# Two layers of masked graph attention: both layers' scores as neighbours, and two vector steps in other places

## The chip, the cores and the metric

The kernel runs on one core of a Trainium2 chip. The metric is the device time of one execution in microseconds (us). A core has five engines that run side by side, each through its own list of instructions in order, and wait for each other by semaphores: TensorE (PE in the profile; its weight loads are PEld), VectorE (DVE), ScalarE (ACT), GpSimd (POOL) and SyncE (SP), which issues the transfers.

## The reference

There are 64 graphs of 256 nodes with 512 features. Layer 0 normalizes the rows, applies a ReLU, maps the rows (`m`), and makes two things from `m` for each of 8 heads of width 64: a softmax over scaled scores of `q` and `k`, and a 0/1 adjacency from cosines of the unit vectors of `m`. Their product weighs the messages. Layer 1 is masked attention with 4 heads. Both layers add to the input. Cut to what matters here:

```python
h = relu(layernorm(x))
m = h @ map_w.T + map_b                        # split into 8 heads of 64
n = m / max(norm(m), 1e-8)
cos_adj = (n @ n.T) * ~mask > 0.1              # "cosines", "unit vectors"
q, k = m @ q_w.T + q_b, m @ k_w.T + k_b
p = softmax(where(mask, -1e10, q @ k.T / 8)) * keep
adj = cos_adj * p
x = x + relu((adj @ (h @ gcn_map_w.T + gcn_map_b)) @ gcn_W.T / (adj.sum(-1) + 1))
h = relu(layernorm(x))                         # layer 1: 4 heads of 64
x = x + softmax(where(mask, q1 @ k1.T / 8, -big)) @ v1 @ Wo + bo
```

Here `mask` is true where a pair is left out in layer 0, and layer 1 takes the pairs the other way round.

## The kernel before

Everything is in 32-bit floats. The kernel is one long list written out by hand: `manual_schedule` keeps each engine's instructions in the order of the Python calls. The function `period(i)` is called for i = 0 to 64. In one period four graphs are at work at different stages: `b` (graph i-1) does its layer 1 attention, `g` (graph i) its layer 0 attention and the projections of its layer 1, `nx` (graph i+1) its layer 0 map, messages, queries and keys, and `n2` (graph i+2) is normalized and turned. In periods 1 to 62 `b`, `g` and `nx` all exist; period 0 has no `b`, period 63 no `nx`, and period 64 only `b`.

Some parts that the change and the profile's rows touch:

- **Products with seven instead of eight blocks.** `seven_products` (L260 to L327) multiplies 2 x 2 blocks with seven products, and is a generator: each `next` issues one step. Three of the products go one after the other into the same PSUM bank, called `z`. Each of the later two may start only when VectorE has read what the bank held: after the first, `out(0, 0, ...)` (L301, shown as mT<-p_m_z,u2p_m for the map), after the second, the sum u4 (L321, uup_m for the map, uup_q for the queries). The map, the messages, the queries and the keys are such products (p_m, p_s, p_q, p_k).
- **Scores.** `products` (L401) makes scores (tile sc) for two heads at a time from 64 rows each, into two PSUM banks; `exps` (L408, ScalarE) empties them into e. All PSUM tiles come from one ring of eight banks in the order of allocation.
- **Masks and half sums.** `masked` (VectorE) multiplies the exponentials by the mask: L415 in layer 1, L417 in layer 0, four calls of 128 x 1024 each period. `halves` (GpSimd, L421) adds the two halves of each, for the sums of the softmax. `off_edges` does both for the listed pairs of heads of layer 0.
- **Cosines.** `spread` sends the inverse norms over DRAM to all partitions of nT, `units` (VectorE, L384) multiplies them with mT in place, and `cosines` (L438) multiplies nT with itself. Only the upper blocks are computed; `far_off` (L448, L451) applies them, sends the block off the diagonal through a transposing transfer, and `far_back` (L463, "turned pass") applies the turned block later, followed by an add on GpSimd (L465).

In `period` before, the order around the change was: scores of layer 1, their masks and half sums; first step of the map (`next(m)`, p_m into bank p_m_24); scores of layer 0; first step of the messages (p_s); masks of the first two pairs of heads; second step of the map, which holds the first z product; third mask; the further steps; cosines. The unit vectors of `nx` were made at the very end of the period before, and the turned passes stood each ahead of a step of the queries or messages.

Of the kernel before, what the change touches and what calls it, by code (L numbers as in the profile page):

```python
# [147 lines left out]
def fast_path(ctx, tc, a, w, chk, out):  # L148
# [8 lines left out]
    H0, NKC = D // DH, D // P  # L157
# [16 lines left out]
    def bank(name, shape=(P, 2, S), dtype=F32):  # L174
        return ring.tile(list(shape), dtype, tag="bank", name=name)
# [175 lines left out]
    def halved(g):  # L351
        g.left_m = left_factors(g.mT, "sm", g.i)
# [29 lines left out]
    def units(g):  # L382

        nc.vector.tensor_mul(g.nT, g.nT, g.mT)  # L384
# [10 lines left out]
    def products(rows, cols, c, name):  # L395

        ps = [bank(f"{name}_{s}", [P, NT, S]) for s in range(2)]
        for j in range(NT):
            for s in range(2):
                h = slice(s * DH, (s + 1) * DH)  # L400
                nc.tensor.matmul(ps[s][:, j, :], rows[h, c, j * P:(j + 1) * P], cols[h, c, :], start=True, stop=True)  # L401
        return ps

    def exps(ps, name):

        e = sb2.tile([P, 2, NT * S], F32, tag="e", name=f"e{name}", bufs=6)
        for s, p in enumerate(ps):
            nc.scalar.activation(e[:, s, :], p.rearrange("p j q -> p (j q)"), AF.Exp, scale=SCALE)  # L408
        return e

    def masked(e, mask, edges):

        m = mask.rearrange("p j q -> p (j q)")[:, None, :].to_broadcast([P, 2, NT * S])
        if edges:
            nc.vector.scalar_tensor_tensor(e, m, 0.5, e, op0=ALU.is_lt, op1=ALU.mult)  # L415
        else:
            nc.vector.tensor_mul(e, e, m)  # L417

    def halves(e, name):
        d = sb2.tile([P, 2, S], F32, tag="d", name=f"d{name}", bufs=6)  # L420
        nc.gpsimd.tensor_add(d, e[:, :, :S], e[:, :, S:])  # L421
        return d
# [133 lines left out]
    def period(i):  # L556
        g = graphs.get(i) if i < B else None
        b, nx, n2 = graphs.get(i - 1), graphs.get(i + 1), graphs.get(i + 2)
        def off_edges(cs):
            for c in cs if g else ():  # L560
                masked(g.e[c], g.mask, edges=False)
                g.d[c] = halves(g.e[c], f"0_{i}_{c}")


        if b:
            b.e1 = [exps(products(b.k1T, b.q1T, c, f"sc1_{b.i}_{c}"), f"1_{b.i}_{c}") for c in range(NIC)]
            for c in range(NIC):
                masked(b.e1[c], b.mask, edges=True)
            if b.last:
                for t in range(NT):  # L570
                    values_in(b, t)
            else:
                b.d1 = [halves(b.e1[c], f"1_{b.i}_{c}") for c in range(NIC)]
        if nx:
            m, s = mapped(nx), messages(nx)
            next(m)
        if g:
            for c in range(NKC):
                g.e[c] = exps(products(g.kT, g.qT, c, f"sc0_{i}_{c}"), f"0_{i}_{c}")
        if nx:  # L580
            next(s)
        off_edges((0, 1))
        if nx:
            next(m)
        off_edges((2,))
        if nx:
            next(m)
            next(s)
            next(m)
            halved(nx)  # L590

        if g:
            for c in range(NKC):
                far_off(g, c, cosines(g, c))
                if c == 0:
                    off_edges((3,))
            for c in range(NKC):
                far_added(g, c)
        if n2:
            shifts(n2, f"0_{n2.i}")  # L600
        if nx:
            q = queries(nx)
            next(q)
            next(s)
        if n2:
            sent(n2, f"0_{n2.i}", 0)
        if nx:
            next(q)
            squares(nx)
            next(s)  # L610
        if n2:
            sent(n2, f"0_{n2.i}", 1)
        for c in range(NKC):
            if g:
                far_back(g, c)
            if nx and c < 3:
                next((q, s, q)[c])
        if nx:
            lengths(nx, norms(nx))

        if i == 0:
            w.finish_seven(w.wqk1)
        if b:
            sums1(b)
            values1(b)
        if g:
            g.avs = sb1.tile([P, NKC, S], F32, tag="wide", name=f"avs{i}")
            g.sms = sb1.tile([P, S], F32, tag="sms", name=f"sms{i}")
            values(g, 0)
            values(g, 1)  # L630
            sums(g)
        if n2:
            joined(n2, f"0_{n2.i}")
            join(n2, 0)
        if nx:
            k = keys(nx)
            next(k)
        if b:
            nc.scalar.activation(b.rz, b.rz, AF.Copy, accum_out=chk[:, b.i, 3:4])
        if g:  # L640
            sums_back(g)
            heads_back(g)
        if n2:
            join(n2, 1)
        if nx:
            next(k)
        if n2:
            edges(n2)
        if b:
            divided(b)  # L650
        if g:
            moments(g, f"1_{i}")
        if nx:
            next(k)
        if g:
            deviations(g)
        if g:
            normalized(g, f"1_{i}")
        if nx:
            nc.scalar.activation(nx.rn, nx.rn, AF.Sqrt)  # L660

        nc.scalar.activation(spare[:, 1:], spare[:, :1], AF.Exp)
        if b:
            for t in range(NT):
                result(b, t)
                if b.last:
                    nc.sync.dma_start(out=out_t[b.i][:, t], in_=b.xs[:, t])
            if not b.last:
                nc.sync.dma_start(out=out_t[b.i], in_=b.xs)
        if i + 3 < B:  # L670
            graphs[i + 3] = load(i + 3)
        if g:
            g.h1T = turned(g, f"1_{i}", "wide")
            j = queries_keys1(g)
            for t in range(NT):
                nc.gpsimd.tensor_add(g.xs[:, t, :], g.xs[:, t, :], w.bo_b)
        if nx:
            next(k)
        if g:
            next(j)  # L680
        if nx:
            nc.vector.reciprocal(nx.rn, nx.rn)
            spread(nx)
        if g:
            next(j)
        if g:
            next(j)
            if not g.last:
                values_in(g, 0)
            next(j)  # L690
        if n2:
            n2.left_h = left_factors(n2.hT, "sh", n2.i)
        if i + 3 < B:
            moments(graphs[i + 3], f"0_{i + 3}")
        if g and not g.last:
            values_in(g, 1)
        if nx:
            units(nx)

    def normal_input(g):  # L700
        g.hT = turned(g, f"0_{g.i}", "hT")
# [2 lines left out]
    with tc.manual_schedule():  # L704
        spare = small.tile([P, 2], F32, tag="spare", name="spare", bufs=1)
        nc.vector.memset(spare, 0.0)
        graphs = {0: load(0)}
        w.load_map()
        gws = [sb2.tile([P, 2, D], F32, tag="e", name=f"gw{k}", bufs=6) for k in range(2)]
        w.load_folded(gws)  # L710
        w.load_scores()
        graphs.update({n: load(n) for n in range(1, min(3, B))})
        w.load_rest()

        def normal(n):
            moments(graphs[n], f"0_{n}")
            deviations(graphs[n])
            normalized(graphs[n], f"0_{n}")

        g = graphs[0]  # L720
        normal(0)
        normal_input(g)
        edges(g)
        w.finish_seven(w.wm)
        m = mapped(g)
        next(m)
        next(m)
        w.fold(gws, bank, w.put_seven)
        next(m)
        w.finish_seven(w.wq)  # L730
        next(m)
        halved(g)
        squares(g)
        w.finish_seven(w.wk)
        q, k, s = queries(g), keys(g), messages(g)
        next(q)
        lengths(g, norms(g))
        w.fold_bias(sb2.tile([P, NKC, P], F32, tag="xn", name="gbb"), bank)
        w.finish_seven(w.wc)
        for step in (k, q, k, q, k, q, k):  # L740
            next(step)
        nc.scalar.activation(g.rn, g.rn, AF.Sqrt)
        nc.vector.reciprocal(g.rn, g.rn)
        spread(g)
        if B > 1:
            edges(graphs[1])
            normal(1)
        nc.scalar.activation(spare[:, 1:], spare[:, :1], AF.Exp)
        for _ in range(5):
            next(s)  # L750
        units(g)
        if B > 1:
            normal_input(graphs[1])
        if B > 2:
            moments(graphs[2], "0_2")
        for i in range(B + 1):
            period(i)
# [298 lines left out]
```

## Time and profile before

| what | value |
|---|---|
| time, median of 3 runs (lowest, highest) | 3695.86 us (3694.76, 3696.32) |
| span of the profiled execution | 3695.8 us |
| one period in the middle, from score product to score product | 56.58 us |
| TensorE busy | 3651.0 us (99%) |
| VectorE, GpSimd, ScalarE busy | 75%, 64%, 52% |
| mean granted TensorE clock | 0.996 |

A row of the timeline gives the start, the length, the engine, the line of the kernel, the operation, what it writes and reads, the shapes, and how many instructions in a row are merged; in brackets stands how long the engine was idle before, and whom it waited for. Matmuls overlap, so a group's cost is the distance from its start to the start of the next group. A 32-bit matmul is recorded as two passes.

### The profile page before, as it was taken

How to read it: one execution, taken by the hardware profiler on the slowest of the kernel's cores; microseconds unless marked ns; L12 is line 12 of the kernel's file. 1: busy time of each engine (PE TensorE's matmuls, PEld its weight loads, DVE VectorE, ACT ScalarE, POOL GpSimd, SP SyncE). 2: the span in 40 equal slices, each digit the busy share in tenths (PEclk: the TensorE clock that was granted, in tenths of full speed). 3: DMA queues.
4: the chain of work that ended last, by engine and by line, in shares of the span. 5: the costliest groups of instructions: out<-in, count | busy, mean ns of one | idle time of the engine just before them, and what ended most of it. 6: DMA issues, size and time to landing. Idle time of an engine off the chain costs nothing.

```text
span 3695.8 us, 76415 instructions
## 1 busy us (share of the span) xinstructions
PE 3651.0 (99%) x29153; PEld 3091.7 (84%) x29153; DVE 2774.1 (75%) x5288; ACT 1904.1 (52%) x4480; POOL 2348.0 (64%) x2044
## 2 busy tenths in 40 slices
PE   7999999999999999999999999999999999999997
PEld 7888888888888888888888888888888888888885
DVE  6777777777777777777877777777777777777775
ACT  3555555555555555555555555555555555555543
POOL 3667566666665665666766666666666667566663
PEclk9999999999999999999999999999999999999998
DMA  3111211211211112112112121121121112211211
GB/s 109 46 50 50 57 44 54 60 42 53 56 47 54 45 53 59 43 53 59 43 54 51 50 57 44 53 60 43 52 56 46 54 47 52 58 43 53 60 29 35
DMA packets 361008, 191.71 MB, mean 52 GB/s; under 512 B 272449, under 2 KB 326977, under 8 KB 360641
## 3 DMA queue, kind: packets, MB, share of 16 engines
q1 hardware_dynamic: 358368, 186.76, 19.0%
q8 instruction: 232, 3.80, 0.4%
q14 instruction: 136, 1.11, 0.1%
q10 hardware_dynamic: 2272, 0.04, 0.0%
HBM read 94.67 MB, written 34.34 MB: 35 GB/s over the span
## 4 chain that ended last, share of the span: by engine, by line
PE 96%; DVE 1%; DMA 1%; POOL 0%; issue 0%; ACT 0%; SPq 0%; DVEq 0%; ACTq 0%; POOLq 0%
PE sc L401 9%; PE av L428 9%; PE p_k L276 6%; PE p_q L276 6%; PE p_m L276 6%; PE p_qk L276 6%; PE p_s L271 6%; PE p_o L553 6%; PE p_v L520 6%; PE p_q_z L276 5%; PE co L438 5%; PE p_qk_z L276 5%; PE p_k_z L276 5%; PE p_m_z L276 5%; PE p_s_z L271 4%; PE sm L481 2%
## 5 line engine op out<-in xcount | busy, mean ns | idle before, releaser
L421 POOL TENSOR_TENSOR d<-e 128x512 f32<-128x512 f32 x382 | 716.2, 1900 | 199.5 <-DVE e L415 191.6
L408 ACT ACTIVATE e<-sc 128x512 f32<-128x512 f32 x768 | 389.9, 620 | 382.1 <-PE sc L401 375.6
L417 DVE TENSOR_TENSOR e<-e,mask 128x1024 f32<-128x1024 f32 x256 | 465.0, 1836 | 55.0 <-ACT e L408 55.0
L506 POOL TENSOR_TENSOR xs<-xs,o 128x512 f32<-128x512 f32 x128 | 188.5, 1494 | 385.5 <-DVE o L504 385.5
L465 POOL TENSOR_TENSOR d<-d,e 128x512 f32<-128x512 f32 x252 | 321.3, 1275 | 170.9 <-DVE e L463 169.2
L254 POOL TENSOR_TENSOR sh<-hT 128x256 f32<-128x256 f32 x128 | 93.6, 731 | 495.1 <-ACT hT L217 317.8
L458 POOL TENSOR_TENSOR d<-d,e 128x512 f32<-128x512 f32 x252 | 312.2, 1268 | 0.0
L451 DVE SCALAR_TENSOR_TENSOR e<-co,e 128x256 f32<-128x256 f32 (+1 forms) x1024 | 282.0, 343 | 35.8 <-ACT up L448 34.7
L448 ACT ACTIVATE up<-co,below 128x128 bf16<-128x128 f32 x512 | 159.6, 366 | 183.2 <-PE co L438 177.4
L553 PE MATMUL p_o<-wo,own 128*128 128x512 f32 x512 | 234.0, 600 | 9.8 <-DVE own L548 9.8
L520 PE MATMUL p_v<-wv,hT 128*128 128x256 f32 x1024 | 242.2, 379 | 0.0
L401 PE MATMUL sc<-qT,kT 64*128 64x256 f32 x2048 | 238.3, 382 | 0.0
L428 PE MATMUL av<-e,sem 128*64 128x256 f32 x2048 | 232.7, 380 | 0.0
L463 DVE SCALAR_TENSOR_TENSOR e<-far,e 128x256 f32<-128x256 bf16 x256 | 230.9, 903 | 0.0
L401 PEld LDWEIGHTS sc<-qT,kT 64*128 64x128 f32 x2048 | 192.9, 187 | 27.5
L428 PEld LDWEIGHTS av<-e,sem 128*64 128x64 f32 x2048 | 147.1, 137 | 75.2 <-DVE e L463 1.1
L491 DVE RECIPROCAL r<-rt 128x16 f32<-128x16 f32 x64 | 16.5, 258 | 253.3 <-PE rt L489 253.3
L520 PEld LDWEIGHTS p_v<-wv,hT 128*128 128x128 f32 x1024 | 184.9, 190 | 20.2 <-issue 0.3
L194 DVE BATCH_NORM_STATS2 st<-xs 128x6 f32<-128x512 f32 x256 | 173.8, 679 | 25.1 <-POOL xs L506 22.1
L438 PE MATMUL co<-nT 64*128 64x256 f32 (+1 forms) x2048 | 184.9, 330 | 0.0
L553 PEld LDWEIGHTS p_o<-wo,own 128*128 128x128 f32 x512 | 93.6, 193 | 104.7 <-issue 101.7
L231 ACT ACTIVATE xn<-xs,shift,rs 128x512 f32<-128x512 f32 x124 | 100.5, 810 | 156.1 <-POOL d L458 153.6
(198 smaller groups left out, 9350.0 us busy)
## 6 DMA issues: line engine op xcount, KB each, us to landing
xs<-in_x_dram SPq DMA_DIRECT2D x64, 512.0 KB
nT<-by_rn SPq DMA_DIRECT2D x128, 256.0 KB
out_dram<-xs SPq DMA_DIRECT2D x63, 512.0 KB
own<-by_rz SPq DMA_DIRECT2D x128, 128.0 KB
ad<-in_adj_dram SPq DMA_DIRECT2D x64, 64.0 KB
far<-up SPq DMA_TRANSPOSE x256
turn<-flat SPq DMA_TRANSPOSE x248
mask<-adb SPq DMA_TRANSPOSE x128
```

What stands on the lines that cost most here:

```text
L271: nc.tensor.matmul(region, src[:, c, :], wt[:, block, c, :], start=p not in opened, stop=True, skip_group_check=True)
L276: nc.tensor.matmul(region[:, f, :], wt[:, block, c, f * P:(f + 1) * P], src[:, c, :], start=p not in opened, stop=True, skip_group_check=True)
L401: nc.tensor.matmul(ps[s][:, j, :], rows[h, c, j * P:(j + 1) * P], cols[h, c, :], start=True, stop=True)
L408: nc.scalar.activation(e[:, s, :], p.rearrange("p j q -> p (j q)"), AF.Exp, scale=SCALE)
L417: nc.vector.tensor_mul(e, e, m)
L421: nc.gpsimd.tensor_add(d, e[:, :, :S], e[:, :, S:])
L428: nc.tensor.matmul(av[s * DH:(s + 1) * DH, n, :], vs[:, j, (h0 + s) * DH:(h0 + s + 1) * DH], q[:, s, j * S:(j + 1) * S], start=(j == 0), s ...
L438: nc.tensor.matmul(ps[s][:, j, j * P:], g.nT[h, c, j * P:(j + 1) * P], g.nT[h, c, j * P:], start=(j == 0), stop=True, skip_group_check=True)
L458: nc.gpsimd.tensor_add(g.d[c], g.d[c], g.e[c][:, :, :S])
L465: nc.gpsimd.tensor_add(g.d[c], g.d[c], g.e[c][:, :, S:])
L520: nc.tensor.matmul(g.p_v[:, t, :], g.h1T[:, c, t * P:(t + 1) * P], w.wv1[:, c, :], start=(c == 0), stop=(c == NKC - 1))
L553: nc.tensor.matmul(p, b.avs1[:, c, t * P:(t + 1) * P], w.wo1[:, c, :], start=(c == 0), stop=(c == NIC - 1))
```

## The change

It makes three moves and adds or removes no instruction. The scores of layer 0 are issued directly behind those of layer 1, ahead of the masks of layer 1 in the list, and the map's first step comes after both. The unit vectors of `g` are made in its own period, behind the masks of the first two pairs of heads, instead of at the end of the period before. Each turned pass stands behind the step of queries or messages that it stood ahead of. The first move lets TensorE do products of one shape in one stretch, the second clears VectorE ahead of the masks, and the third lets sums that TensorE waits for go ahead of the turned passes.

```diff
         if b:
             b.e1 = [exps(products(b.k1T, b.q1T, c, f"sc1_{b.i}_{c}"), f"1_{b.i}_{c}") for c in range(NIC)]
+        if g:
+            for c in range(NKC):
+                g.e[c] = exps(products(g.kT, g.qT, c, f"sc0_{i}_{c}"), f"0_{i}_{c}")
+        if b:
             for c in range(NIC):
                 masked(b.e1[c], b.mask, edges=True)
...
         if nx:
             m, s = mapped(nx), messages(nx)
             next(m)
-        if g:
-            for c in range(NKC):
-                g.e[c] = exps(products(g.kT, g.qT, c, f"sc0_{i}_{c}"), f"0_{i}_{c}")
-        if nx:
             next(s)
         off_edges((0, 1))
+        if g:
+            units(g)
         if nx:
             next(m)
         off_edges((2,))
...
         for c in range(NKC):
+            if nx and c < 3:
+                next((q, s, q)[c])
             if g:
                 far_back(g, c)
-            if nx and c < 3:
-                next((q, s, q)[c])
         if nx:
             lengths(nx, norms(nx))
...
         if g and not g.last:
             values_in(g, 1)
-        if nx:
-            units(nx)
...
         for _ in range(5):
             next(s)
-        units(g)
         if B > 1:
             normal_input(graphs[1])
```

## The prediction

> Times are microseconds. "+x" is a position in a period, counted from the first score product of layer 1.
>
> **What bounds the kernel now.** I read the page first: shares of the engines, and the chain that ended last.
>
> ```profile
> PE 3651.0 (99%) x29153; PEld 3091.7 (84%) x29153; DVE 2774.1 (75%) x5288; ACT 1904.1 (52%) x4480; POOL 2348.0 (64%) x2044
> ...
> PE 96%; DVE 1%; DMA 1%; POOL 0%; issue 0%; ACT 0%; SPq 0%; DVEq 0%; ACTq 0%; POOLq 0%
> ```
>
> TensorE is the chain. The other engines matter only where TensorE waits for them, and the waits of the page are nearly all of other engines for TensorE. So I read TensorE's timeline over one period in the middle (1813.46 to 1870.04, 56.58 long). Columns: start, length, instruction, count; a matmul is recorded as two passes. What a group costs is the distance to the next group's start.
>
> ```profile
> 1813.46 2.00 PE L401 MATMUL sc<-qk 64*128 64x256 f32 x16
> 1815.39 2.05 PE L276 MATMUL p_m<-hT,wm 128*128 128x128 f32 x16
> 1817.37 3.72 PE L401 MATMUL sc<-qT,kT 64*128 64x256 f32 x32
> 1821.02 1.13 PE L271 MATMUL p_s<-wc,hT 128*128 128x256 f32 x4
> ...
> 1824.67 1.06 PE L276 MATMUL p_m_z<-sh,wm 128*128 128x128 f32 x8
> ...
> 1840.06 1.16 PE L276 MATMUL p_q_z<-sm,wq 128*128 128x128 f32 x8
> ```
>
> The map's first products take 1.98 between two score groups (64 rows), while sixteen such products elsewhere take 1.78 (p_qk, 1803.66 to 1805.44). The four p_s after scores take 0.97, elsewhere 0.87 (1825.56 to 1826.43). So every step between 64-row and 128-row products costs about 0.2: half at the last product before it, half behind the first one after it.
>
> The last period with scores has no next graph. Its two score groups are already neighbours, as the change makes them everywhere:
>
> ```profile
> 3624.48 2.00 PE L401 MATMUL sc<-qk 64*128 64x256 f32 x16
> 3626.31 3.62 PE L401 MATMUL sc<-qT,kT 64*128 64x256 f32 x32
> ```
>
> They take 1.83 and 3.46 (the next group starts at 3629.77), against 1.93 and 3.65 in the middle: nothing between them, and no wait for a PSUM bank.
>
> The same period shows VectorE (masks, L417) and GpSimd (half sums, L421) once all exponentials are there. One instruction per row:
>
> ```profile
> 3628.13 2.18 POOL L421 TENSOR_TENSOR d<-e 128x512 f32<-128x512 f32 x1 [8.00 <-DVE e L415]
> 3629.10 2.29 DVE L417 TENSOR_TENSOR e<-e,mask 128x1024 f32<-128x1024 f32 x1
> 3630.27 2.25 POOL L421 TENSOR_TENSOR d<-e 128x512 f32<-128x512 f32 x1
> 3631.32 2.28 DVE L417 TENSOR_TENSOR e<-e,mask 128x1024 f32<-128x1024 f32 x1
> 3632.48 2.24 POOL L421 TENSOR_TENSOR d<-e 128x512 f32<-128x512 f32 x1
> 3633.52 2.28 DVE L417 TENSOR_TENSOR e<-e,mask 128x1024 f32<-128x1024 f32 x1
> ```
>
> Alone a mask takes 1.22 (3636.78, the fourth) and a half sum 1.27. Here each takes 2.2 to 2.3, and each ends about 1.1 after the one before it on the other engine: they take turns.
>
> Last, the waits of TensorE's weight loads hold one row of this path, 0.29 in every period:
>
> ```profile
> PEld p_q_z L276 <- DVE uup_q L321: 18.1, 63, 0.3
> ```
>
> [...]
>
> **The change part by part.**
>
> *Scores together.* Before, the four groups of the fence take 1.93 + 1.98 + 3.65 + 0.97 = 8.53. After: 1.83 + 3.46 + 0.10 for leaving + (1.98 - 0.10, since p_s needs no switch) + 0.87 = 8.14. Gain 0.39 in each of the 62 periods that have a previous, a present and a next graph. Period 0 has two score edges either way. The exponentials come every 0.49 (eight in 4.03, one 0.62) against 0.43 a bank for the products, and the ring of eight absorbs the difference, as in the last period.
>
> *Turned passes one step later.* Now uup_q (1839.59 to 1840.01) stands behind the first far_back (0.41). The p_s_z before it takes 0.92 instead of 0.87, and p_q_z 1.09 instead of 0.98 (the map's third z product, 1826.43 to 1827.41, which also ends in a switch): 0.16 lost. Without far_back ahead, uup_q still waits for its product: the map's twin uup_m starts 0.27 after its p_s group, uup_q 0.45 after. I take a start 0.13 earlier; bounds 0.11 and 0.16. Gain 0.13. The far_back passes then end where they did, since VectorE does the same work; GpSimd's last add ended at 1846.19 and is wanted from 1847.48 on.
>
> *Unit vectors behind the second mask.* This is L384, 1.21 long, two SBUF inputs:
>
> ```profile
> 1815.38 1.21 DVE L384 TENSOR_TENSOR nT<-nT,mT 128x1024 f32<-128x1024 f32 x1
> ...
> 1823.21 0.41 DVE L301 TENSOR_TENSOR mT<-p_m_z,u2p_m 128x256 f32<-128x256 f32 x1
> ```
>
> Today it runs while GpSimd is idle (1814.85 to 1817.81) and VectorE would wait for exponentials anyway; at its new place GpSimd has a half sum waiting at every moment. Queued behind it is mT<-p_m_z, which frees the bank for the second z product of the map, and behind that the third mask and uup_m, which frees it for the third.
>
> VectorE after, from the last period (masks of layer 1 at +2.34 there, since the first exponentials end them, not L384): layer 0's masks issue at +4.62 and +6.84; the third instruction, a mask there, runs +9.04 to +11.32. In the new kernel the units stand third, of the same size. So units end at +11.32, mT<-p_m_z at +11.65. In the middle of the kernel before that was 1823.62, or +10.16.
>
> TensorE after: scores end at +5.39, the map's first products +7.27, p_s +8.14, first z +9.03, p_m +10.82 (1.79, as 1822.88 to 1824.67). There the second z product is due; before it was due at +11.21. From uup_q's end at 1840.01 with 0.16 lost, a sum must end 0.17 before its product is due: +10.65. It is 1.00 late.
>
> Then the third mask: [...]the mask until +13.53, uup_m until +13.87. The third z product is due at 10.82 + 1.00 + 0.89 + 0.87 = +13.58, so the sum at +13.41. It is 0.46 late. Everything behind shifts with TensorE; VectorE's gaps of 1.52 and 4.02 later in the period take up the rest.
>
> Sum for a period: 1.00 + 0.46 - 0.39 - 0.13 = +0.94; 62 of them +58. In the last score period the cosines need the units, and the third mask ends one turn pair (2.2) later: +2. In period 0 VectorE has no layer 1 masks and the units are done in time: 0; the prologue's L384 is hidden. 3695.9 + 60 = 3756. Bounds: 0 to 0.46 for the second lateness (it needs two turns in the order I assume), 0.9 to 1.1 for the first.
>
> **The rivals.**
> - *The units cost nothing on the path*, because GpSimd gives way or VectorE's earlier start suffices: -0.52 x 62, 3664. For it: masks of layer 1 start 0.7 earlier (+2.34 against 1816.52, or +3.06), and a gap of 0.85 at 1818.86 closes. Against it: with 1.21 without any turn the units end only if no half sum comes between, and six rows in turn show one each time. 10%.
> - [...]units end +10.20, mT +10.53, in time; the half sum until +11.33, third mask +12.41, uup_m +12.76, for a product due at +12.58, 0.34 late. 0.34 - 0.52 = -0.18 a period, with the tail 3687. For it: a mask in period 0 followed a mask at once (2.36 for two), but no half sum was waiting then. 7%.
> - *Only the first lateness*: 1.00 - 0.52 = +0.48, 3728. 8%.
>
> **How the numbers follow.** The forecast has 75%, the rivals 10, 7 and 8. The range holds the forecast and the third rival, 83%: from 3724 to 3770, the top being the forecast with no gain from the turned passes (+8) and 0.1 more lateness (+6). Faster: the first two rivals, 17%. Same: 2%, taken from between the cases. Slower 81%.
>
> **What would show it.** Right: p_m of the first products at 1.88, p_s 0.87; no wait row of p_q_z for uup_q; L384's mean near 2.2 instead of 1.2; new rows of TensorE waiting at p_m_z for mT or uup_m, about 1.4 in all per period; a period of 57.5. Wrong: L384 still at 1.2, or a period of 56.06 with p_m_z never waiting.[...]

## The result, and the profile after

The changed kernel takes 3755.53 us (median of 6 runs, 3753.0 to 3756.56), the kernel before 3695.25 beside it (6 runs, 3690.99 to 3696.32). The ratio is 1.0164, with a 95% interval of 1.0151 to 1.0177: 1.6% slower, where 3756 was forecast.

The page after begins with the span; then the engines' shares and, further down, the chain that ended last:

```profile
span 3754.1 us, 76480 instructions
...
PE 3645.6 (97%) x29153; PEld 3094.6 (82%) x29153; DVE 2857.4 (76%) x5288; ACT 1904.1 (51%) x4480; POOL 2358.4 (63%) x2044
...
PE 80%; DVE 14%; issue 3%; ACT 2%; DMA 0%; POOL 0%; DVEq 0%; SPq 0%; ACTq 0%; POOLq 0%
```

TensorE is busy for 5 us less and idle for 64 more. VectorE is busy for 83 us more with the same number of instructions, and its share of the chain goes from 1% to 14%. So the chain now leaves TensorE for VectorE: in 61 of the 62 full periods it runs through the unit vectors, and the timeline shows where.

This is TensorE in the period that corresponds to the one shown of before:

```profile
1841.74 2.00 PE L401 MATMUL sc<-qk 64*128 64x256 f32 x16
1843.58 3.62 PE L401 MATMUL sc<-qT,kT 64*128 64x256 f32 x32
1847.13 2.05 PE L276 MATMUL p_m<-hT,wm 128*128 128x128 f32 x16
1849.01 1.03 PE L271 MATMUL p_s<-wc,hT 128*128 128x256 f32 x4
1849.88 1.05 PE L276 MATMUL p_m_z<-hT,wm 128*128 128x128 f32 x8
1850.77 1.95 PE L276 MATMUL p_m<-sh,wm 128*128 128x128 f32 x16
1853.69 1.16 PE L276 MATMUL p_m_z<-sh,wm 128*128 128x128 f32 x8 [0.97 <-DVE mT L301]
1854.69 1.03 PE L271 MATMUL p_s<-wc,hT 128*128 128x256 f32 x4
1855.68 1.16 PE L276 MATMUL p_m_z<-sh,wm 128*128 128x128 f32 x8
1856.77 2.89 PE L438 MATMUL co<-nT 64*128 64x256 f32 x32
```

Up to 1850.77 each group is as cheap as hoped: both score groups 5.39 (1841.74 to 1847.13), the map's first products 1.88, p_s 0.87. Then TensorE stands idle for 0.97 ahead of the second z product, and what is next in its list does not go first: p_s, which writes another bank, starts at 1854.69, 1.00 after the late product. What is behind the wait runs a little wide: z 1.00 instead of 0.89, p_s 0.99 instead of 0.87, the third z 1.09 instead of 0.98.

VectorE over the same stretch:

```profile
1844.09 2.36 DVE L415 SCALAR_TENSOR_TENSOR e<-mask,e 128x1024 f32<-128x1024 bf16 x2 [0.34 <-ACT e L408]
1846.37 4.50 DVE L417 TENSOR_TENSOR e<-e,mask 128x1024 f32<-128x1024 f32 x2
1850.79 2.29 DVE L384 TENSOR_TENSOR nT<-nT,mT 128x1024 f32<-128x1024 f32 x1
1853.21 0.42 DVE L301 TENSOR_TENSOR mT<-p_m_z,u2p_m 128x256 f32<-128x256 f32 x1
1853.60 1.69 DVE L417 TENSOR_TENSOR e<-e,mask 128x1024 f32<-128x1024 f32 x1
1855.21 0.41 DVE L321 TENSOR_TENSOR uup_m<-p_m_z,u5p_m 128x256 f32<-128x256 f32 x1
```

The unit vectors (L384) take 2.29, not 1.21 as before, and behind them is the sum that the second z product waits for. Their view over the whole execution shows that they are never done in less (shortest, median and longest in ns):

```profile
L384 DVE TENSOR_TENSOR nT<-nT,mT x64: 2277/2284/2291, 68.3 to 3692.0; 128x1024 f32<-128x1024 f32 x64
```

The waits (waiter, whom for; sum in us, times, longest) have a new row of weight loads for mT, and the row for uup_m was 1.5 in 3 times before; the row of p_q_z is shorter than its 18.1 of before but not gone:

```profile
PEld p_m_z L276 <- DVE mT L301: 72.0, 62, 1.4
...
PEld p_m_z L276 <- DVE uup_m L321: 23.3, 63, 0.8
PEld p_q_z L276 <- DVE uup_q L321: 11.3, 63, 0.2
```

The period is 57.54, against 56.58. From the first score product of layer 1 in period 1 to that in period 63 are 62 periods, 3508.8 us before and 3567.5 after: +58.7, which is all of the 58.3 by which the span grew.

### The profile page after: what moved, and what is told of

The parts are those of the page before. It is cut to its first block, busy times and chain, and to the rows that moved or that the text cites. A ratio compares the mean times of both kernels' runs of the same rounds, so it can differ in the third digit from the quotient of the medians.

```text
span 3754.1 us, 76480 instructions
## 1 busy us (share of the span) xinstructions
PE 3645.6 (97%) x29153; PEld 3094.6 (82%) x29153; DVE 2857.4 (76%) x5288; ACT 1904.1 (51%) x4480; POOL 2358.4 (63%) x2044
## 4 chain that ended last, share of the span: by engine, by line
PE 80%; DVE 14%; issue 3%; ACT 2%; DMA 0%; POOL 0%; DVEq 0%; SPq 0%; ACTq 0%; POOLq 0%
PE av L428 9%; PE p_k L276 6%; PE p_q L276 6%; PE p_qk L276 6%; PE p_o L553 6%; PE p_v L520 6%; PE co L438 5%; DVE e L417 5%; PE p_q_z L276 5%; PE p_qk_z L276 5%; PE p_k_z L276 5%; PE p_s_z L271 4%; PE p_s L271 4%; PE p_m_z L276 4%; DVE e L415 4%; DVE nT L384 4%
## 5 line engine op out<-in xcount | busy, mean ns | idle before, releaser
L417 DVE TENSOR_TENSOR e<-e,mask 128x1024 f32<-128x1024 f32 x256 | 510.1, 2012 | 0.7 <-ACT e L408 0.7
L276 PE MATMUL p_m_z<-sh,wm 128*128 128x128 f32 x1024 | 148.0, 287 | 60.9 <-DVE mT L301 60.2
L276 PEld LDWEIGHTS p_m_z<-sh,wm 128*128 128x128 f32 x1024 | 123.9, 191 | 95.5 <-DVE mT L301 72.0
L463 DVE SCALAR_TENSOR_TENSOR e<-far,e 128x256 f32<-128x256 bf16 x256 | 189.6, 760 | 0.6 <-DMA far<-up 0.6
```

The costliest lines, as they stand in the source:

```text
L276: nc.tensor.matmul(region[:, f, :], wt[:, block, c, f * P:(f + 1) * P], src[:, c, :], start=p not in opened, stop=True, skip_group_check=True)
```

## The experiments

My theory: the joined scores and the later turned passes gain (0.39 and about 0.13 a period), and the move of the unit vectors loses 1.46, because at their new place VectorE and GpSimd take turns, one whole instruction each: 2.29 there for the units, 1.21 before. The rivals: the loss lies elsewhere in the new order (the three moves disturb one another); the units' own place in the queue is at fault and not the turns; the sum waits for a buffer and not for the engine. Each time is a median, each ratio is against the kernel before on the same chip.

**Each part by itself.** First the change without the move of the unit vectors.

```diff
-        if g:
-            units(g)              # behind off_edges((0, 1))
...
+        if nx:
+            units(nx)             # end of period, as before
...
+        units(g)                  # ahead of period 0, as before
```

> The changed kernel with the unit vectors back at the end of the period before; scores together and turned passes later stay. Theory (the two late sums on the map's z bank come only from the unit vectors standing in the turns of VectorE and GpSimd): both waits vanish, 0.39 + 0.11 are gained in 62 periods, about 3664 us, and no row of TensorE waiting at p_m_z for mT. Rival (bringing the scores together makes VectorE late by itself, since all six half sums then fall into turns with the masks): the waits at p_m_z stay in part, 3720 to 3755 us.

Measured: 3661.3 (3660.47 to 3662.24), ratio 0.9909, 0.9894 to 0.9924. The period is 56.08. VectorE there makes the units ahead of the masks, at single length, and the sum is early:

```profile
1797.60 1.21 DVE L384 TENSOR_TENSOR nT<-nT,mT 128x1024 f32<-128x1024 f32 x1
1798.73 2.35 DVE L415 SCALAR_TENSOR_TENSOR e<-mask,e 128x1024 f32<-128x1024 bf16 x2
1801.00 4.51 DVE L417 TENSOR_TENSOR e<-e,mask 128x1024 f32<-128x1024 f32 x2
1805.43 0.41 DVE L301 TENSOR_TENSOR mT<-p_m_z,u2p_m 128x256 f32<-128x256 f32 x1
```

TensorE reaches its second z product 0.6 after that sum has ended, with no wait:

```profile
1804.70 1.95 PE L276 MATMUL p_m<-sh,wm 128*128 128x128 f32 x16
1806.48 1.06 PE L276 MATMUL p_m_z<-sh,wm 128*128 128x128 f32 x8
```

So the loss comes with the move of the unit vectors, and without it the other two beat the kernel before by 0.9%. No kernel here that leaves nothing out is faster.

Then the scores alone: e1 with the turned passes where they were.

```diff
         for c in range(NKC):
-            if nx and c < 3:
-                next((q, s, q)[c])
             if g:
                 far_back(g, c)
+            if nx and c < 3:
+                next((q, s, q)[c])
```

> Only the scores as neighbours, the unit vectors and the turned passes as before. Theory (each step between 64-row and 128-row products costs 0.2, two of four steps go): a score stretch of 5.38 instead of 1.93 + 3.65, p_m 1.88, p_s 0.87, 0.39 x 62, about 3671 us. Rival (the steps cost nothing, the gaps were waits for exponentials that reappear): 3695 us.

Measured: 3672.22 (3670.42 to 3674.1), ratio 0.9939, 0.9926 to 0.9953; period 56.18. The turned passes alone are the opposite edit of the same lines, on the kernel before:

> Only the turned passes one step later. Theory: uup_q starts earlier, p_q_z loses 0.05 instead of 0.16 as in the changed kernel, 0.11 x 63, about 3688.5 us. Rival (the turned passes are wanted by the weighing or by the sums, and their lateness costs what the step wins): 3695 us or more, with a wait at av or sm.

Measured: 3688.78 (3687.49 to 3690.2), ratio 0.9981, 0.9975 to 0.9988; period 56.47. In its timeline p_s_z now takes 0.87 and p_q_z 1.03, instead of 0.92 and 1.09:

```profile
1832.78 1.03 PE L271 MATMUL p_s_z<-wc,sh 128*128 128x256 f32 x4
1833.65 1.10 PE L276 MATMUL p_q_z<-sm,wq 128*128 128x128 f32 x8
1834.68 0.64 PE L362 MATMUL p_n<-sq,blk 128*32 128x256 f32 x8
```

And the units alone, on the kernel before:

```diff
         off_edges((0, 1))
+        if g:
+            units(g)
...
-        if nx:
-            units(nx)
...
-        units(g)
```

> The kernel before with only the unit vectors moved behind the masks of the first two pairs. Theory (turns): layer 1's half sums are done before layer 0's first mask, but a half sum still comes ahead of the unit vectors; they end at about +11.4, the first sum is 0.9 late and the second 0.2, with the longer due time of the old score order; 1.15 x 62, about 3768 us. Rival (the unit vectors hurt only together with the joined scores, because only then do all half sums pile up): 3695 us.

Measured: 3772.23 (3768.54 to 3774.79), ratio 1.0209, 1.0192 to 1.0226; period 57.80. Its waits:

```profile
PEld p_m_z L276 <- DVE mT L301: 55.9, 63, 1.2
...
PEld p_m_z L276 <- DVE uup_m L321: 25.0, 63, 0.8
```

The two gains add up: -0.40 (e2) and -0.11 (e3) make e1's -0.50. The units cost 1.22 in the old order and 1.46 in the new one, where the third z product is due 0.39 earlier and VectorE lets it start only about 0.15 earlier (+13.93 against +14.08, medians over the periods). So the moves do disturb one another, by 0.24 a period, but most of the loss is there without the others, and the rival is out as its main cause.

**Is it the turns?** If GpSimd's work is the cause, taking it away must bring the units to 1.2 at their new place. This kernel is the changed one without GpSimd's half sums and the adds to them; a tile of ones stands for them, so the softmax denominators are left out.

```diff
 def halves(...)
-        d = sb2.tile([P, 2, S], F32, tag="d", name=f"d{name}", bufs=6)
-        nc.gpsimd.tensor_add(d, e[:, :, :S], e[:, :, S:])
-        return d
+        return fixed
...
-            nc.gpsimd.tensor_add(g.d[c], g.d[c], g.e[c][:, :, :S])
+            pass
...
-        if not g.last:
-            nc.gpsimd.tensor_add(g.d[c], g.d[c], g.e[c][:, :, S:])
```

> The changed kernel without GpSimd's half sums and the adds to them: a fixed tile of ones stands in for all of them, so the softmax denominators are left out; TensorE has the same products. Theory (the unit vectors are late because a half sum of GpSimd takes its turn before each VectorE instruction): the unit vectors take 1.2 again, end before +8.5 of the period, the waits at p_m_z vanish, about 3664 us. Rival (they are late by their place in VectorE's list and by the sum's wait for their read of mT, whatever GpSimd does): waits of 1.4 a period stay, about 3755 us.

Measured: 3661.17 (3660.43 to 3661.73), ratio 0.9909, 0.9894 to 0.9924, as e1. The units:

```profile
L384 DVE TENSOR_TENSOR nT<-nT,mT x64: 1214/1219/1222, 65.5 to 3596.0; 128x1024 f32<-128x1024 f32 x64
```

and in the timeline of VectorE the sum behind them now waits for its product, not the other way round:

```profile
1801.56 1.22 DVE L384 TENSOR_TENSOR nT<-nT,mT 128x1024 f32<-128x1024 f32 x1
1804.01 0.42 DVE L301 TENSOR_TENSOR mT<-p_m_z,u2p_m 128x256 f32<-128x256 f32 x1 [1.23 <-PE p_m_z L276]
1804.35 1.22 DVE L417 TENSOR_TENSOR e<-e,mask 128x1024 f32<-128x1024 f32 x1
```

With GpSimd's half sums gone, the place in the queue costs nothing. The two masks ahead of the units are shorter here too (2.35 together instead of 4.50): the units start at +6.83 instead of +9.05 and end at +8.05 instead of +11.33, so of the 3.3 that they are earlier 2.2 come from the masks and only 1.1 from the units' own turn. If a turn goes by the instruction and not by its length, the same work as two halves must cost more than as one:

```diff
-        nc.vector.tensor_mul(g.nT, g.nT, g.mT)
+        for c in (slice(0, 2), slice(2, 4)):
+            nc.vector.tensor_mul(g.nT[:, c], g.nT[:, c], g.mT[:, c])
```

> The changed kernel with the unit vectors as two instructions of half the size at the same place. Theory (a turn costs by the instruction, not by its length): a half sum comes ahead of each half, so the first sum is due at +10.65 and done at about +13.05, 2.4 late; the third mask then finds no half sum waiting and the second sum is in time; 2.4 instead of 1.47 a period, about 3812 us. Rival (the two engines share by length, two halves cost what one whole does): about 3755 us.

Measured: 3836.19 (3834.66 to 3840.59), ratio 1.0384, 1.0367 to 1.0402. The stretch of the units is as expected: each half takes 1.75, and from the start of the first to the end of the second are 3.42 instead of 2.29. The third mask behind them takes 1.21, alone, and the third z product is in time.

```profile
L385 DVE TENSOR_TENSOR nT<-nT,mT x128: 1744/1750/1756, 65.2 to 3772.4; 128x512 f32<-128x512 f32 x128
```

The waits show the second z product waiting, and nearly nothing else:

```profile
PEld p_m_z L276 <- DVE mT L301: 143.5, 63, 2.7
```

But the time is 24 above what was expected. Of its 62 periods 47 are 58.4 to 58.8 long, as this wait makes them, and 15 are 60.0 to 60.4. 15 x 1.6 is the 24. In such a long period some products behind the wait take about twice their time (timeline of TensorE):

```profile
420.17 1.28 PE L276 MATMUL p_m_z<-sh,wm 128*128 128x128 f32 x8 [2.39 <-DVE mT L301]
421.25 1.92 PE L271 MATMUL p_s<-wc,hT 128*128 128x256 f32 x4
422.95 1.79 PE L276 MATMUL p_m_z<-sh,wm 128*128 128x128 f32 x8
```

and the granted clock says why (columns: stretch and its length; busy time and number of instructions of TensorE, its weight loads, VectorE, ScalarE and GpSimd; granted clock; share of the DMA engines; GB/s):

```profile
419.00:421.00 2.00, 0.83 (x7) 0.83 (x8) 1.87 (x3) 0.00 (x0) 0.01 (x1) 1.00 0.00 0
421.00:424.50 3.50, 3.50 (x15) 3.14 (x14) 1.85 (x5) 0.00 (x0) 1.27 (x1) 0.51 0.00 0
424.50:428.00 3.50, 3.50 (x38) 3.08 (x38) 2.66 (x7) 2.28 (x8) 2.30 (x4) 1.00 0.08 19
```

From 0.9 after the end of the wait TensorE gets half its clock for 3.4 us, 0.51 over the stretch. So the wait costs a second time in these periods; the last section shows in which.

**Is it the buffer of mT?** The sum mT<-p_m_z writes the tile that the units read, so in the program it comes after them; in the changed kernel it starts at 1853.21, 0.13 after their end. Two such tiles take this away. To make room, this kernel reads the output's bias from the tile of the messages' bias (both are zero) and makes some small tiles smaller or lets them share room.

```diff
-        g.mT = sb1.tile([P, NKC, S], F32, tag="mT", name=f"mT{g.i}")
+        g.mT = sb1.tile([P, NKC, S], F32, tag="mT", name=f"mT{g.i}", bufs=2)
```

> The changed kernel with two buffers for mT, so that the sum mT<-p_m_z need not wait for the unit vectors' read of the old mT. Room for it comes from smaller or shared tiles elsewhere; layer 1's output bias is read from the messages' bias tile, both zero here. Theory (the third mask's turn sets the end of the second sum, so what the first sum wins the second one loses): the sum starts 0.2 earlier, the second wait grows by as much, 3755 us. Rival (the wait for the read is part of the loss): 15 us less, about 3740 us.

Measured: 3759.1 (3757.11 to 3762.5), ratio 1.0176, 1.0159 to 1.0193; the period stays at 57.54. The sum now starts 0.08 before the recorded end of the units (1851.18, 1851.26), and the waits move from the first sum to the second:

```profile
PEld p_m_z L270 <- DVE mT L295: 58.5, 62, 1.2
...
PEld p_m_z L270 <- DVE uup_m L315: 37.1, 63, 0.8
```

With two tiles the units can also stand behind the sum, which is then in time:

```diff
         off_edges((0, 1))
-        if g:
-            units(g)
         if nx:
             next(m)
+        if g:
+            units(g)
```

> As the kernel with two mT buffers, and the unit vectors stand behind the first sum mT<-p_m_z instead of ahead of it. Theory (each VectorE instruction of this kind costs a turn of 2.2 wherever it stands ahead of the third mask, and the third mask's end at +13.5 sets the third z product): the first wait vanishes and the second grows to about 1.45, again 3755 us. Rival (only the place ahead of the first sum hurts): the second wait stays at 0.2 to 0.5, about 3680 to 3695 us.

Measured: 3758.91 (3757.09 to 3761.5), ratio 1.0172, 1.0155 to 1.0189; the period is again 57.54. Its timeline shows the whole wait one product later:

```profile
1852.71 1.06 PE L270 MATMUL p_m_z<-sh,wm 128*128 128x128 f32 x8
1853.61 1.03 PE L265 MATMUL p_s<-wc,hT 128*128 128x256 f32 x4
1855.83 1.16 PE L270 MATMUL p_m_z<-sh,wm 128*128 128x128 f32 x8 [1.20 <-DVE uup_m L315]
```

Three arrangements of the units and the sums are late by 1.24 + 0.23 (the changed kernel), 1.01 + 0.45 (e6) and 0 + 1.46 (e7). They give one period, because in each of them uup_m stands behind the same masks and units with the same turns: it ends at +13.87 or +13.88, and the third z product waits for it. So the loss is set by what stands ahead of that last sum in VectorE's queue, and the buffer is out as a cause. No run left the units at their new place and moved GpSimd's half sums instead, so whether that would keep the two gains is open.

## Why the prediction was right

- *Scores together.* Forecast 0.39 a period; the stretch of 5.39, the 1.88 and the 0.87 came as worked out, and e2 measured 0.40. The neighbours in the last period were a fair sample of what the change makes everywhere.
- *Turned passes one step later.* Forecast 0.13 with bounds 0.11 to 0.16; measured 0.11 (e3). uup_q starts earlier, but the wait for it is 0.05 a period instead of 0.16, not 0: the forecast's sign that this row would vanish was wrong.
- *Unit vectors behind the second mask.* The weakest step, the order in which the two engines take their turns, held in all 62 periods. In the period shown, the units end at +11.33 (forecast +11.32), the third mask at +13.54 (+13.53), uup_m at +13.88 (+13.87). In the rival with the other order, forecast at 3687, they would end at +10.20. That a turn is a whole instruction long is what e4 (1.22 without the half sums) and e8 (two halves, two turns, 3.42) show. Who is next when both wait was my estimate from six rows. In the traces of before and after, a mask, the units or a half sum ended 946 times while an instruction of the other engine among these was under way, and each time the next to end was the other engine's. Why the two engines alternate is not shown.
- *The split of the two waits* was off. The first was 1.24, not 1.00, the second 0.23, not 0.46. I had let mT<-p_m_z follow the units without a gap, as a mask would (the units start 0.08 before the recorded end of the mask ahead of them); since it overwrites what they read, it starts 0.13 after their end and itself ends at +11.89, not +11.65. e6, where that tie is gone, measures 1.01 and 0.45. The end of uup_m alone sets the sum of both, so this error had no effect on the total: 1.47 measured against 1.46.
- *Tail and prologue.* The forecast had +2 and 0. The third mask of the last score period did end 2.2 later and its cosines waited, but from the start of period 63 to the end the kernel is not slower (71.1, before 71.3). Before, a wait near the same place was followed by attention products at half clock (16 in 3.68 instead of 1.95; granted clock 0.50 from 3635.36 to 3642.19); after, the half clock (0.50 from 3690.73 to 3697.56) fell on the cosines (4.46, in the middle of the kernel 2.89). The forecast didn't have this. Its tail was 2 us too high and its periods together less than 1 too low, and the runs of one kernel lie up to 5 us apart: that the total came to within 1 us is in part luck; +0.94 forecast and 58.7 / 62 = +0.95 measured a period are not.

The rival that looked best beforehand, units that cost nothing, gives 3664, and this is what e1 and e4 measure: right about the gain, but only with the units at their old place or the half sums gone.

## What to carry to other kernels

Before an instruction moves to a place where "the engine has time", look what the other engines do there: the unit vectors took 1.21 us beside an idle GpSimd and 2.29 among its half sums, with no row of their waiting for GpSimd to show it, only a longer mean. When a late sum holds TensorE, find the last of the sums in the queue that TensorE needs; reordering the ones before it moved the wait and not the time. And take a change of several moves apart, since here two gained 0.9% of the time and one lost 2.5%.

## What the hardware showed unexpectedly

TensorE waits in all of e8's 62 periods, for 2.10 us in nearly all, and 15 of these waits are followed by half clock for 3.4 us: the mean clock of the profiled execution is 0.990 in e8 and 0.995 or 0.996 in all other kernels. Which 15 they are can be read from the trace. In it the half clock lies on one grid of 3.413 us; in the traces of before and after all changes of the granted clock lie on such a grid, to within 0.001. The period of 58.4 is no multiple of that, so the wait falls at another place of the grid each time. Here are two waits of nearly the same length:

```profile
2304.02 1.16 PE L276 MATMUL p_m_z<-sh,wm 128*128 128x128 f32 x8 [2.10 <-DVE mT L301]
...
2422.52 1.16 PE L276 MATMUL p_m_z<-sh,wm 128*128 128x128 f32 x8 [2.11 <-DVE mT L301]
```

And these are the stretches of the grid in which they lie and the ones behind (columns: stretch and its length; busy time and number of instructions of TensorE; granted clock; share of the DMA engines; GB/s):

```profile
2301.82:2305.23 3.41, 1.31 (x10) 1.00 0.00 0
2305.23:2308.65 3.42, 3.42 (x14) 0.50 0.02 5
...
2417.87:2421.28 3.41, 2.54 (x23) 1.00 0.00 0
2421.28:2424.70 3.42, 2.18 (x15) 1.00 0.00 0
2424.70:2428.11 3.41, 3.41 (x39) 1.00 0.00 0
```

The first wait lies in one stretch, which leaves TensorE idle for 2.10 of its 3.41, and the next stretch gets half clock. The second is split, 0.87 and 1.24, and the clock stays. It is so without exception in e8 from 120 to 3700 us: each of the 15 stretches at full clock with at least 1.93 idle was followed by half clock, and none of the 1019 with at most 1.92. In the traces of before and after, each with its own grid of 3.413, the stretches at full clock that half clock followed (7 and 6) were idle for at least 2.17, and every other one for at most 1.72. The waits of 0.97 in the changed kernel brought no half clock: from 63 to 3690 us its granted clock is 1.00. In e7, with waits of 1.20, the mean clock of the profiled execution is 0.995. These idle times are as exact as the ends of the matmuls, which the profile models. What decides the clock is not shown by these counts.
